# A fused four-layer graph kernel: the set-up before the first tile in another order

## The chip, the cores and the metric

The kernel runs on one NeuronCore of one Trainium2 chip. The metric is the device time of one execution in microseconds, as a median of several runs. The core has a tensor engine (PE; its weight loads are listed apart, as PEld), a vector engine (DVE), a scalar engine (ACT), GpSimd (POOL) and a sync engine (SP) that does nothing but start transfers. Each engine takes its instructions strictly in the order in which they were written for it, and waits where an operand or a buffer isn't ready. ACT can start transfers too; while it does, it computes nothing.

## The reference

For 64 graphs with N = 256 nodes and 128 features, x has the shape 64 x 256 x 128, and all graphs share one 256 x 256 matrix `adj`. Four layers follow one another, each of the form x = x + layer(relu(layernorm(x))). The start of the kernel concerns the first alone:

```python
W1, W2 = (W[:, :F], W[:, F:])          # W is adj, F = 128
s1 = jnp.einsum('bkf,ef->bke', x, W1)
s2 = jnp.einsum('bkf,ef->bke', x, W2)
pre = s1[:, :, None, :] + s2[:, None, :, :] + b_lin
h = jnp.where(pre >= 0, pre, ALPHA * pre)
e = jnp.einsum('bije,e->bij', h, a) + bias   # bias is adj too
attn = jax.nn.softmax(e, axis=2)
out = jax.nn.sigmoid(jnp.einsum('bij,bjf->bif', attn, x))
```

For each graph, e needs 256 x 256 x 256 leaky-relu values, and these pairwise values are most of the kernel's work. The other three layers are a gated graph layer, an attention with tanh and exp, and five steps of a recurrent gate; their weights are the many small inputs (bi, bn, bm, be, We, Wi, Wn, Wm, q, k, v, w3 to u5).

## The kernel before

**Tiling.** The graphs go in groups of one or two. For a graph, h is layer-normed x (`ln_relu`: bn_stats and bn_aggr on DVE, four small operations on POOL for rstd and shift, the relu on ACT), then it is transposed on PE (`transpose_blocks`), and two products with W give s1 (receivers, with the bias b_lin) and s2 (senders). A negative copy of s1, s1n, serves the engines that write the relu as a maximum. `Pairs` then goes through 32 rows of eight receivers each. A batch is eight tiles of 128 x 256; three engines make batches in different forms: ACT by a relu with s1 as bias (L620), POOL by min and max with s1n (L625), DVE by a maximum over a half batch at once (L608). PE multiplies each batch by the window `a_win`, which holds signs, and adds it to `e_ps` (L673). ACT and DVE keep their own copies of s2 in PSUM (`s2_act`, `s2_dve`). The batches lie in ten buffers (`r`); a buffer is free again once PE has read it. Where PE has five batches waiting, a row's second half is merged into the first by DVE (L642), which saves PE a batch.

**Set-up.** The order of W's rows is chosen by the sign of `a`. `constants0` computes it: sgn, then five small matmuls that count signs (`before_ps`), then eight tiny DVE operations that give each row its place, then a scaled permutation matrix `perm` (four DVE operations, L264). Four matmuls apply it to adj (`w_p_ps`), and the result is copied to `w_p`, whose half 0 makes s1 and whose half 1 makes s2. Aside from that way, `a_rep` and `v2_ps` give `v2_rep`, with which each e_ps is opened; `odd_ps` holds the permuted bias and a count, and feeds `blin_p` and `blin_n`; `left_ps` and `bounds` give a correction that the softmax of each graph needs (`adj_l`). `constants1` prepares the later layers' weights.

**Transfers.** Before any of this, the program starts its loads. SP takes x of the first group, x of the second, thirteen weights and x of the third. ACT takes twelve: adj, a, b_lin, bi, bn, the broadcasts of bm and be, and five biases.

**Order.** `tc.manual_schedule()` leaves the order to the code. A planner (the loop at the end) keeps one clock for each engine in nanoseconds, `model.t`, which the priced calls `dve(n)`, `act(n)`, `pool(ns)` and `mm` advance. The work apart from the tiles is in five chains of Python generators: `ahead` (heads and senders of coming graphs), `behind` (softmax), `chain3`, `chain12` and `chain4` (set-up and later layers). Each `yield` names the engine of the next piece, and may name a condition and an earliest time. The loop takes whatever can start earliest by the clocks: a piece of a chain, a half batch of tiles, a merge, or a product of PE. A piece can start when the piece before it in its chain is done, plus a lag (300 ns after PE, 150 DVE, 170 ACT, 200 POOL); if `paced` is set, it also waits for a due time, which grows by the chain's pace (1500 for `ahead`, 2400 for `chain3`) with each piece, from 300 on. Tiles are dealt once `s2` of a graph is in `sent`: from then on, any of ACT, DVE and POOL whose clock is lowest takes the next half batch. So the planner decides on paper; the chip only carries out the order.

All clocks begin at 0, and no clock knows of the time that transfers take to land. Before the change `paced` holds from the first moment (until the last two graphs). The price of a 128 x 256 tile is 357 on ACT and 453 on POOL, a DVE half batch 1131, a batch on PE 858.

Of the kernel before, what the change touches and what calls it, by code (L numbers as in the profile page):

```python
# [8 lines left out]
F32 = mybir.dt.float32  # L9
# [3 lines left out]
P = 128  # L13
# [6 lines left out]
BUFS = 10  # L20
SPARE = 5
MARGIN = {"pe": 300}
MEMORY = 7000
LAG = {"pe": 300, "dve": 150, "act": 170, "pool": 200}

# [5 lines left out]
def sizes(xt):  # L31

    blocks = xt.shape[1]
    return blocks, blocks // 2, blocks * P
# [19 lines left out]
def kernel(ctx: ExitStack, tc: tile.TileContext, ins: dict, out: bass.AP):  # L54
# [18 lines left out]
    def psum(shape, name):  # L73
        return ps_b.tile(shape, F32, tag="ps_b", name=name)
# [4 lines left out]
    def psum_h(shape, name):  # L79
        return ps_h.tile(shape, F32, tag="ps_h", name=name)  # L80
# [17 lines left out]
    def mm(out, lhsT, rhs, **flags):  # L98


        n = 1
        for d in rhs.shape[1:]:
            n *= d
        model.op("pe", max(n, 64) * 1.676)
        for c in range(4):
            nc.tensor.matmul(  # L106
                out[bass.ts(c, 32), :], lhsT=lhsT[:, bass.ts(c, 32)], rhs=rhs, **flags
            )
# [22 lines left out]
    def fetch(shape, name, source, queue=nc.sync, t=None):  # L131
        t = t or constant(shape, name)
        queue.dma_start(out=t, in_=source)
        return t

    def column(name):

        v = ins[name]
        return fetch(
            [P, v.shape[0] // P], "c_" + name, v.rearrange("(c p) -> p c", p=P), nc.scalar  # L140
        )

    order = ctx.enter_context(tc.manual_schedule())
    xts = [load_x(0)]
    adj_n = fetch([P, 2, N], "adj_n", adj.rearrange("(c p) m -> p c m", p=P), nc.scalar)
    a_col = column("L0_gnn_a")
    blin = column("L0_gnn_b_lin")
    ident = constant([P, P], "ident")
    make_identity(nc, ident)
    neg_half = constant([P, 4], "neg_half")  # L150
# [59 lines left out]
    def constants0():  # L210
# [13 lines left out]
        dve(2).scalar_tensor_tensor(a_abs, a_col, -1.0, a_col, ALU.mult, ALU.max)  # L224
        for c in range(2):
            dve(P).tensor_scalar(
                a_rep[:, c, :], a_rep[:, c, :], a_col[:, c : c + 1], None, ALU.mult
            )
# [9 lines left out]
        v2_ps = psum([P, P], "v2_ps")  # L238
        for c in range(2):
            mm(  # L240
                v2_ps, lhsT=adj_n[:, c, P : 2 * P], rhs=a_rep[:, c, :],
                start=(c == 0), stop=(c == 1),
            )
        yield "dve"
        bef = constant([P, 3], "bef")
        dve(3).tensor_copy(bef, before[:, 0:3])
        n_pos = bef[:, 2:3]
# [14 lines left out]
        for src in range(2):  # L262
            for c, size in ((0, a_abs), (1, a_abs1)):
# [13 lines left out]
        act(2 * N).copy(w_p, p)  # L277
        counts["w_p"] += 1
        yield "dve"
        dve(P).tensor_copy(v2_rep, v2_ps)  # L280

# [9 lines left out]
        p = psum([P, 4], "odd_ps")  # L291
        mm(p[:, 0:1], lhsT=ones, rhs=odd, start=True, stop=True)
        for c in range(2):
            for src in range(2):
                mm(
                    p[:, 1 + c : 2 + c], lhsT=perm[:, src, c, :], rhs=blin[:, src : src + 1],
                    start=(src == 0), stop=(src == 1),
                )
        yield "dve"
        dve(2).tensor_copy(blin_p, p[:, 1:3])  # L300
        dve(2).tensor_scalar(blin_n, p[:, 1:3], -1.0, None, ALU.mult)
        counts["w_p"] += 1
        odd_all = constant([P, 1], "odd_all")
        dve(1).tensor_copy(odd_all, p[:, 0:1])
# [101 lines left out]

    def ln_relu(space, xt, tag, ln, when=None):

        G = xt.shape[1]
        for g in range(G):
            if g % 2 == 0:
                yield "dve", when
# [16 lines left out]
        pool(302).tensor_tensor(shift, minus, rstd, ALU.mult)  # L431
        for g in range(G):
            if g % 2 == 0:
                yield "act"
            if g == 0:
                h = space.tile([P, G, P], F32, tag=ln, name=tag, bufs=3 if space is ap else 1)
            act(P, 2, 1).activation(  # L437
                h[:, g, :], xt[:, g, :], AF.Relu, bias=shift[:, g : g + 1],
                scale=rstd[:, g : g + 1],
            )  # L440
        return h

    def transpose_blocks(space, src, tag, banks):
# [8 lines left out]
        act(W).copy(t, tp)  # L452
        return t


    def head(xt, to):
        G, _, W = sizes(xt)
# [47 lines left out]
    def senders(b, of, to):  # L505

        h_t = flat(of["h_t"][:, 2 * b : 2 * b + 2, :])
        yield "pe"
        p = psum_h([P, 2, N], "s2_ps")
        for ec in range(2):  # L510
            mm(p[:, ec, :], lhsT=w_p[:, 1, bass.ts(ec, P)], rhs=h_t, start=True, stop=True)
        yield "act"
        s2 = ap.tile([P, 2, N], F32, tag="s2", name="s2")
        act(2 * N).copy(s2, p)
        to["s2"] = s2
# [13 lines left out]
        to["adj_l"] = adj_l  # L529
# [536 lines left out]
            ahead.add(senders(graphs[n + 1][1], made[graphs[n + 1][0]], sent[n + 1]))  # L1066

    chain3.add(constants0())
    ahead.add(head(xts[0], made[0]))
    ahead.add(senders(0, made[0], sent[0]))  # L1070
    ahead.add(head(xts[1], made[1]))
    n = 0
    while True:
        paced = n < len(graphs) - 2
        if not making and n < len(graphs) and "s2" in sent[n]:
            g, b = graphs[n]
            making.append(Pairs(g, b, made[g], sent[n]))
            multiplying.append(making[0])
            begin(n)
            n += 1  # L1080
# [92 lines left out]
```

## Time and profile before

| What | us |
| --- | --- |
| median of three runs | 5151.03 (5151.01 to 5160.24) |
| the profiled execution, its own time | 5146.78 |
| span of the profiled execution | 5144.3 |
| first product of PE on set-up data (`before_ps`) | 4.89 |
| table load of ACT | 10.18 to 11.46 |
| first tile of ACT, POOL, DVE | 23.59, 23.66, 24.51 |
| last pairwise work, about | 5050 |

The page is read as follows: times are in us from the start of the span; "busy" leaves out time spent in issuing transfers and in waiting. Matmul ends are modelled, so a busy PE is not a PE at its peak. In a line of the order of time, the number in brackets is the time for which the engine stood idle before, and after the arrow stands what ended it. Instructions of one kind that follow one another are one line with a count. PE splits each f32 product in four column groups and two instructions each, so that one `mm` shows as eight.

### The profile page before, as it was taken

How to read it: one execution, taken by the hardware profiler on the slowest of the kernel's cores; microseconds unless marked ns; L12 is line 12 of the kernel's file. 1: busy time of each engine (PE TensorE's matmuls, PEld its weight loads, DVE VectorE, ACT ScalarE, POOL GpSimd, SP SyncE). 2: the span in 40 equal slices, each digit the busy share in tenths (PEclk: the TensorE clock that was granted, in tenths of full speed). 3: DMA queues.
4: the chain of work that ended last, by engine and by line, in shares of the span. 5: the costliest groups of instructions: out<-in, count | busy, mean ns of one | idle time of the engine just before them, and what ended most of it. 6: DMA issues, size and time to landing. Idle time of an engine off the chain costs nothing. (4 is left out here: it accounts for less than half of the span.)

```text
span 5144.3 us, 172484 instructions
## 1 busy us (share of the span) xinstructions
PE 5063.0 (98%) x66800; PEld 2358.0 (46%) x66800; DVE 4983.5 (97%) x9900; ACT 5032.0 (98%) x13224; POOL 4895.6 (95%) x10829
## 2 busy tenths in 40 slices
PE   8999999999999999999999999999999999999997
PEld 4545444436444444544444544544444444444443
DVE  7999999999999999999999999999999999999994
ACT  7999999999999999999999999999999999999994
POOL 8999999999999999999999999999999999999992
PEclk9999999999999999999999999999999999999999
DMA  0000000000000000000000000000000000000000
GB/s 21 6 2 5 5 6 6 6 2 6 6 6 6 2 6 6 6 6 2 6 6 6 6 6 2 6 6 6 6 2 6 6 6 5 2 5 4 4 6 6
DMA packets 56104, 29.32 MB, mean 6 GB/s; under 512 B 20337, under 2 KB 55281, under 8 KB 55281
## 3 DMA queue, kind: packets, MB, share of 16 engines
q1 hardware_dynamic: 53168, 17.97, 1.4%
q8 instruction: 522, 8.55, 0.7%
q14 instruction: 302, 2.47, 0.2%
q10 hardware_dynamic: 2112, 0.33, 0.0%
HBM read 9.84 MB, written 8.45 MB: 4 GB/s over the span
## 5 line engine op out<-in xcount | busy, mean ns | idle before, releaser
L625 POOL TENSOR_SCALAR r<-s,s1n 128x256 f32<-128x256 f32 x10204 | 4646.4, 478 | 102.0 <-PE e_ps L673 33.5
L620 ACT ACTIVATE r<-s_act,s 128x256 f32<-128x256 f32 x9976 | 4593.6, 1478 | 10.5 <-PE e_ps L673 10.4
L673 PE MATMUL e_ps<-r,a_win 128*32 128x512 f32 x27632 | 3379.5, 593 | 9.8 <-POOL r L625 3.4
L642 DVE SCALAR_TENSOR_TENSOR r<-s_dve,s1n,r 128x256 f32<-128x256 f32 x5136 | 2093.8, 471 | 2.0 <-ACT r L620 1.0
L608 DVE TENSOR_TENSOR r<-s_dve,s1n 128x1024 f32<-128x1024 f32 x1735 | 2017.3, 1210 | 7.3 <-PE e_ps L673 1.4
L673 PEld LDWEIGHTS e_ps<-r,a_win 128*32 128x32 f32 x27632 | 1095.3, 110 | 1593.2 <-issue 1124.2
L620 ACT ACTIVATE r<-s,s 128x256 f32<-128x256 f32 x512 | 381.1, 1666 | 0.0
L437 ACT ACTIVATE h<-x,bsh,brs 128x128 f32<-128x128 f32 x384 | 329.8, 1386 | 3.6 <-POOL bsh L431 2.3
L946 ACT ACTIVATE gate_ps<-gate_ps,bz 128x512 f32<-128x512 f32 (+1 forms) x170 | 269.7, 1586 | 5.9 <-PE gate_ps L106 5.9
L948 ACT ACTIVATE hv_ps<-hv_ps,bh 128x512 f32<-128x512 f32 (+1 forms) x170 | 266.4, 1567 | 5.4 <-PE hv_ps L106 5.4
L106 PE MATMUL m_ps<-adj_t,hn 128*32 128x256 f32 x4096 | 268.1, 380 | 2.8 <-ACT hn L968 2.7
L927 ACT COPY m_t<-m_ps 128x512 f32<-128x512 f32 (+1 forms) x170 | 260.9, 1535 | 8.5 <-PE m_ps L106 8.5
L933 ACT ACTIVATE m_ps<-gate_ps,br 128x512 f32<-128x512 f32 (+1 forms) x170 | 256.9, 1511 | 9.2 <-PE gate_ps L106 8.8
L968 ACT COPY hn<-hn_ps 128x512 f32<-128x512 f32 (+1 forms) x136 | 208.1, 1530 | 20.6 <-PE hn_ps L106 20.5
L106 PEld LDWEIGHTS m_ps<-adj_t,hn 128*32 128x32 f32 x4096 | 157.5, 110 | 112.3 <-issue 31.9
L697 ACT ACTIVATE pm<-e_ps,nmax 128x256 f32<-128x256 f32 x128 | 195.0, 1531 | 2.2 <-DVE nmax L688 2.2
L106 PE MATMUL gate_ps<-m_t,t_w_w 128*32 128x512 f32 (+1 forms) x1360 | 187.3, 572 | 8.6 <-ACT m_t L927 7.8
L106 PE MATMUL gate_ps<-m_t,w_t 128*32 128x512 f32 (+1 forms) x1360 | 185.2, 568 | 3.1 <-ACT m_ps L933 3.1
L106 PE MATMUL hv_ps<-m_t,t_w_w 128*32 128x512 f32 (+1 forms) x1360 | 185.0, 567 | 0.0
L106 PE MATMUL hv_ps<-rh,u_th 128*32 128x512 f32 (+1 forms) x1360 | 184.9, 567 | 0.0
L106 PE MATMUL hn_ps<-ident,hf 128*32 128x128 f32 x4096 | 162.9, 274 | 12.5 <-DVE hf L958 12.5
L106 PEld LDWEIGHTS hn_ps<-ident,hf 128*32 128x32 f32 x4096 | 136.4, 110 | 77.0 <-issue 51.3
(206 smaller groups left out, 5951.7 us busy)
## 6 DMA issues: line engine op xcount, KB each, us to landing
xt<-in_x_dram SPq DMA_DIRECT2D x30, 256.0 KB
out_dram<-y SPq DMA_DIRECT2D x30, 256.0 KB
row<-rows SPq DMA_DIRECT2D x128, 0.5 KB
xt<-in_x_dram SPq DMA_DIRECT2D x4, 128.0 KB
out_dram<-y SPq DMA_DIRECT2D x4, 128.0 KB
bound<-row SPq DMA_DIRECT2D x30, 2.0 KB
raw_L_gnn_w_w<-in_L_gnn_w_w_dram SPq DMA_DIRECT2D x3, 128.0 KB
adj_n<-in_adj_dram ACTq DMA_DIRECT2D x1, 256.0 KB
```

The lines of the kernel that those rows point to most:

```text
L106: nc.tensor.matmul(out[bass.ts(c, 32), :], lhsT=lhsT[:, bass.ts(c, 32)], rhs=rhs, **flags)
L437: act(P, 2, 1).activation(h[:, g, :], xt[:, g, :], AF.Relu, bias=shift[:, g : g + 1], scale=rstd[:, g : g + 1],)
L608: nc.vector.tensor_tensor(r[:, 2 * g2 : 2 * g2 + 2, :, :], s2[:, ec : ec + 1, :].unsqueeze(1).to_broadcast([P, 2, 2, N]), self.s1n_v[:, ec ...
L620: nc.scalar.activation(r[:, g, ic, :], s2[:, ec, :], AF.Relu, bias=s1[:, ec, i : i + 1])
L625: nc.gpsimd.tensor_scalar(r[:, g, ic, :], s2[:, ec, :], FLT_MAX, s1n[:, ec, i : i + 1], ALU.min, ALU.max,)
L642: nc.vector.scalar_tensor_tensor(r[:, g, ic, :], self.own("dve")[:, 1, :], self.of["s1n"][:, 1, i : i + 1], r[:, g, ic, :], ALU.max, ALU.add,)
L673: nc.tensor.matmul(self.e_ps[bass.ts(g, 32), :, :].rearrange("p a b -> p (a b)"), lhsT=a_win[:, batch["ec"], 31 - t : 63 - t], rhs=flat(r[ ...
L927: act(W).copy(m_t, m_ps)
L933: act(W, 1).activation(t_r, g_ps, AF.Tanh, bias=br, scale=0.5)
L946: act(W, 1).activation(t_z, g_ps, AF.Tanh, bias=bz, scale=0.5)
L948: act(W, 1).activation(cand, hv_ps, AF.Tanh, bias=bh)
L968: act(W).copy(hn, tp)
```

## The change

Four things are moved, and the planner's start is set in another way.

- **Transfers.** `column` and the two broadcasts go to SP's queue. ACT keeps two: a, which is now first, and adj. b_lin is second on SP, after x of the first group; the other nine stay at their places in the program, behind most of the weights.
- **Table.** A one-column tanh on ACT, on a constant set by DVE, stands right after ACT's two transfers.
- **W.** In `constants0` the a_rep products and `v2_ps` move behind W; the permuted bias gets its own bank and its matmuls stand ahead of W's; W's matmuls run half 1 first; its copy is split in two, one for each half.
- **First group.** `first_head` takes the place of `head` and of the first part of `senders` for the first group: it makes s2 and s1 by four matmuls into two banks, with one wait for the whole of W; s1n is made by DVE, s2 and s1 by ACT.
- **Planner.** x of the first group is taken to land at 3400 ns and a at 3900. Nothing is paced before the first graph's tiles begin. At that moment the clocks of all engines are raised to ACT's.

```diff
-    def column(name):
+    def column(name, queue=nc.sync):
...
     xts = [load_x(0)]
+    a_col = column("L0_gnn_a", nc.scalar)
     adj_n = fetch([P, 2, N], "adj_n", adj.rearrange("(c p) m -> p c m", p=P), nc.scalar)
-    a_col = column("L0_gnn_a")
     blin = column("L0_gnn_b_lin")
+    table = constant([P, 1], "table")
+    nc.vector.memset(table, 0.0)
+    nc.scalar.activation(table, table, AF.Tanh)
...
-    bm_bc = fetch([P, P], "bm_bc", ins["L1_gnn_bm"].partition_broadcast(P), nc.scalar)
-    be_bc = fetch([P, 1], "be_bc", ins["L1_gnn_be"].partition_broadcast(P), nc.scalar)
+    bm_bc = fetch([P, P], "bm_bc", ins["L1_gnn_bm"].partition_broadcast(P))
+    be_bc = fetch([P, 1], "be_bc", ins["L1_gnn_be"].partition_broadcast(P))
...
-        yield "dve"
+        yield "dve", None, LANDS + 500
...
         yield "pe"
+        b_ps = psum([P, 2], "blin_ps")
+        for c in range(2):
+            for src in range(2):
+                mm(
+                    b_ps[:, c : c + 1], lhsT=perm[:, src, c, :], rhs=blin[:, src : src + 1],
+                    start=(src == 0), stop=(src == 1),
+                )
         p = psum([P, 2, N], "w_p_ps")
-        for half in range(2):
+        for half in (1, 0):
...
-        yield "act"
-        act(2 * N).copy(w_p, p)
-        counts["w_p"] += 1
+        yield "dve"
+        dve(2).tensor_copy(blin_p, b_ps)
+        dve(2).tensor_scalar(blin_n, b_ps, -1.0, None, ALU.mult)
+        for half in (1, 0):
+            yield "act"
+            act(N).copy(w_p[:, half, :], p[:, half, :])
+        counts["w_p"] += 2
+        yield "dve"
+        for c in range(2):
+            dve(P).tensor_scalar(
+                a_rep[:, c, :], a_rep[:, c, :], a_col[:, c : c + 1], None, ALU.mult
+            )
+        yield "pe"
...
+    def first_head(xt, to, snd):
+
+        G, _, W = sizes(xt)
+        h = yield from ln_relu(ap, xt, "h0", "h0", at=LANDS)
+        h_t = yield from transpose_blocks(ap, h, "h0t", psum_h)
+        to.update(h=h, h_t=h_t)
+        yield "pe", lambda: counts["w_p"] > 1
+        s2_ps, s1_ps = psum_h([P, 2, N], "s2_ps"), psum_a([P, 2, W], "s1_ps")
+        for half, p in ((1, s2_ps), (0, s1_ps)):
+            for ec in range(2):
+                mm(
+                    p[:, ec, :], lhsT=w_p[:, half, bass.ts(ec, P)], rhs=flat(h_t),
+                    start=True, stop=True,
+                )
+        yield "dve"
+        s1n = ap.tile([P, 2, W], F32, tag="s1n", name="s1n")
+        for ec in range(2):
+            dve(W, 1).tensor_scalar(
+                s1n[:, ec, :], s1_ps[:, ec, :], -1.0, blin_n[:, ec : ec + 1], ALU.mult, ALU.add
+            )
+        yield "act"
+        s2 = ap.tile([P, 2, N], F32, tag="s2", name="s2")
+        act(2 * N).copy(s2, s2_ps)
+        s1 = ap.tile([P, 2, W], F32, tag="s1", name="s1")
+        for ec in range(2):
+            act(W, 1).activation(
+                s1[:, ec, :], s1_ps[:, ec, :], AF.Identity, bias=blin_p[:, ec : ec + 1]
+            )
+        to.update(s1=s1, s1n=s1n)
+        snd["s2"] = s2
...
-    ahead.add(head(xts[0], made[0]))
+    ahead.add(first_head(xts[0], made[0], sent[0]))
...
-        paced = n < len(graphs) - 2
+        paced = 0 < n < len(graphs) - 2
...
             making.append(Pairs(g, b, made[g], sent[n]))
+            if n == 0:
+                model.t = {e: max(t, model.t["act"]) for e, t in model.t.items()}
```

More of the change, by code (lines that the diff above doesn't have):

```diff
@@ L22 @@
 MARGIN = {"pe": 300}
+LANDS = 3400
 MEMORY = 7000
@@ L134, in fetch @@
         return t
-    def column(name):
+    def column(name, queue=nc.sync):
         v = ins[name]
-        return fetch(
-            [P, v.shape[0] // P], "c_" + name, v.rearrange("(c p) -> p c", p=P), nc.scalar
-        )
+        return fetch([P, v.shape[0] // P], "c_" + name, v.rearrange("(c p) -> p c", p=P), queue)
     order = ctx.enter_context(tc.manual_schedule())
     xts = [load_x(0)]
+    a_col = column("L0_gnn_a", nc.scalar)
     adj_n = fetch([P, 2, N], "adj_n", adj.rearrange("(c p) m -> p c m", p=P), nc.scalar)
-    a_col = column("L0_gnn_a")
     blin = column("L0_gnn_b_lin")
+    table = constant([P, 1], "table")
+    nc.vector.memset(table, 0.0)
+    nc.scalar.activation(table, table, AF.Tanh)
     ident = constant([P, P], "ident")
@@ L219, in col @@
             return constant([P, 2], name)
-        yield "dve"
+        yield "dve", None, LANDS + 500
         sgn, a_abs = col("sgn"), col("a_abs")
         dve(2).tensor_scalar(sgn, a_col, 0.0, None, ALU.is_ge)
[L224 to L228, printed above, removed]
         yield "pe"
@@ L235, in constants0 @@
         mm(before[:, 2:3], lhsT=ones, rhs=sgn[:, 1:2], start=False, stop=True)
[L238 to L243, printed above, removed]
         yield "dve"
+        dve(2).scalar_tensor_tensor(a_abs, a_col, -1.0, a_col, ALU.mult, ALU.max)
         bef = constant([P, 3], "bef")
@@ L275, in constants0 @@
                 )
-        yield "act"
-        act(2 * N).copy(w_p, p)
-        counts["w_p"] += 1
+        yield "dve"
[11 more added lines that the diff above has]
+        yield "pe"
+        v2_ps = psum([P, P], "v2_ps")
+        for c in range(2):
+            mm(
+                v2_ps, lhsT=adj_n[:, c, P : 2 * P], rhs=a_rep[:, c, :],
+                start=(c == 0), stop=(c == 1),
+            )
         yield "dve"
@@ L290, in constants0 @@
         yield "pe"
[L291 to L298, printed above, removed]
+        p = psum([P, 1], "odd_ps")
+        mm(p, lhsT=ones, rhs=odd, start=True, stop=True)
         yield "dve"
-        dve(2).tensor_copy(blin_p, p[:, 1:3])
-        dve(2).tensor_scalar(blin_n, p[:, 1:3], -1.0, None, ALU.mult)
-        counts["w_p"] += 1
         odd_all = constant([P, 1], "odd_all")
-        dve(1).tensor_copy(odd_all, p[:, 0:1])
+        dve(1).tensor_copy(odd_all, p)
         left, left_n, left_nb = col("left"), col("left_n"), col("left_nb")
@@ L405, in constants1, with ln_relu @@
                 dve(1).tensor_scalar(t, t, scale, None, ALU.mult)
-    def ln_relu(space, xt, tag, ln, when=None):
+    def ln_relu(space, xt, tag, ln, when=None, at=None):
         G = xt.shape[1]
@@ L413, in ln_relu @@
             if g % 2 == 0:
-                yield "dve", when
+                yield "dve", when, at
             if g == 0:
@@ L453, in transpose_blocks @@
         return t
+    def first_head(xt, to, snd):
[7 more added lines that the diff above has]
+            for ec in range(2):
+                mm(
+                    p[:, ec, :], lhsT=w_p[:, half, bass.ts(ec, P)], rhs=flat(h_t),
[14 more added lines that the diff above has]
+                s1[:, ec, :], s1_ps[:, ec, :], AF.Identity, bias=blin_p[:, ec : ec + 1]
+            )
+        to.update(s1=s1, s1n=s1n)
+        snd["s2"] = s2
     def head(xt, to):
@@ L507, in senders @@
         h_t = flat(of["h_t"][:, 2 * b : 2 * b + 2, :])
[L508 to L515, printed above, removed]
+        if "s2" not in to:
+            yield "pe"
+            p = psum_h([P, 2, N], "s2_ps")
+            for ec in range(2):
+                mm(p[:, ec, :], lhsT=w_p[:, 1, bass.ts(ec, P)], rhs=h_t, start=True, stop=True)
+            yield "act"
+            s2 = ap.tile([P, 2, N], F32, tag="s2", name="s2")
+            act(2 * N).copy(s2, p)
+            to["s2"] = s2
         if "bound" not in of:
```

## The prediction, made before the change was run

> **What bounds the kernel now.** I read the page first, then the first 60 us in order of time, engine by engine, then busy time by stretch and the waits of the first 60 us. The page says that the long middle is full:
>
> ```profile
> PE 5063.0 (98%) x66800; PEld 2358.0 (46%) x66800; DVE 4983.5 (97%) x9900; ACT 5032.0 (98%) x13224; POOL 4895.6 (95%) x10829
> ```
>
> Four engines share one job, so a change can gain only where they are not full: at the two ends. The diff touches only the start. The order of time gives the way to the first tile on ACT, DVE and POOL (columns: start us, us, engine, line, operation, count, idle before and its releaser):
>
> ```profile
> 9.81 0.33 ACTq L133 DMA_DIRECT2D c_L_gnn_u_b<-in_L_gnn_u_b_dram  x1
> 10.18 1.28 ACT L437 ACT_TABLE_LOAD   x1 [10.18 <-DMA c_L_gnn_w_b<-in_L_gnn_w_b_dram]
> 11.47 0.88 ACT L437 ACTIVATE h<-xt,bsh,brs 128x128 f32<-128x128 f32 x2
> 16.58 0.58 ACT L277 COPY w_p<-w_p_ps 128x512 f32<-128x512 f32 x1 [3.04 <-PE w_p_ps L106]
> 22.97 0.59 ACT L514 COPY s<-s_ps 128x512 f32<-128x512 f32 x1 [2.05 <-PE s_ps L106]
> 23.66 29.06 POOL L625 TENSOR_SCALAR r<-s,s1n 128x256 f32<-128x256 f32 x63 [16.82 <-ACT s L514]
> 24.51 3.48 DVE L608 TENSOR_TENSOR r<-s_dve,s1n 128x1024 f32<-128x1024 f32 x3
> ```
>
> ACT issues transfers until 10.14, loads its table, and only then makes h, whose shift POOL had ready at 6.84. PE sits behind h (transposes at 12.02), although the permutation was ready at 8.43. Production starts at 23.6.
>
> The second loss comes after that. Busy time by stretch (sum, instructions in brackets), and the waits of 23.6 to 60:
>
> ```profile
> 23.60:60.00 36.40, 32.95 (x288) 11.73 (x284) 26.19 (x50) 22.24 (x60) 35.99 (x80) 0.95 0.01 2
> 140.00:5050.00 4910.00, 4874.89 (x64286) 2260.15 (x64282) 4840.43 (x9636) 4890.03 (x12858) 4773.89 (x10545) 1.00 0.02 5
> ```
>
> ```profile
> PEld e_ps L673 <- POOL r L625: 16.6, 19, 3.1
> ACT h L437 <- POOL bsh L431: 8.0, 1, 8.0
> DVE adj_t L342 <- PE adj_t_ps L106: 7.3, 1, 7.3
> ```
>
> The columns are PE, PEld, DVE, ACT, POOL. In 36.4 us ACT was idle 14.2 us, DVE 10.2, POOL 0.4; everybody waits for POOL. The planner's clocks explain it. In them nothing before the first tile costs POOL more than the layer norm: due at 3.3 us, 1.8 long, so POOL is free at 5.1, while the same plan has ACT at 20.3 (s2 copy due at 300 + 13 x 1500 ns = 19.8 us) and DVE at 18.0 (due at 300 + 7 x 2400 ns = 17.1, and 0.9 of work). It therefore deals POOL some 15 us of tiles before s2 exists. In truth all three begin at 23.6: POOL is 18.6 us behind its plan, DVE 5.6, ACT 3.3, and PE's fixed order makes the others wait for the difference, 13 and 15 us, which is about the 10.2 and 14.2 idle.
>
> **What the skill says.** "ScalarE: Activation LUTs", What ACT_TABLE_LOAD costs: about 1283 ns a load, plus a drain on a switch. The trace has 1.28 us, once. "DMA: Bandwidth & Descriptors", Issuing engines are not separate DMA queues: a second issuing engine saves only sequencer time. The trace agrees: ACT's loss is issue time. "TensorE: Matmul & The Clock Gate", Part 1: half clock until about 3.4 us of sustained work. Here PE worked from 12.02, its weight loads still came 0.43 us apart per four at 15.44 (the half-rate pace of 256 columns), by 17.22 they were faster, and the granted clock was 0.50 again at 21 to 26. So "about 4 to 5 us" in this trace.
>
> **The change, part by part, up to the first tile.** Order on each engine follows from the planner's own prices, now without due times before the first graph.
>
> 1. ACT's queue: ten of twelve transfers go to SP; ACT keeps the a vector (now first) and adj. That frees ACT from about 1.7 instead of 10.14; table and dummy tanh end by about 3.3, hidden under the wait for x (first bn_stats at 3.49). Cost nothing; uncovered it would be 1.3 + 0.2. On SP the ten add between 10 x 0.33 = 3.3 us and the 8.4 they took on ACT (1.76 to 10.14): the last load goes out at 15.8 to 20.9 instead of 12.5. Queued behind: x(1), first read at 46.9 before; bm's broadcast, read by DVE at 46.2; the row transfer of the bounds at 29.2. All have over 8 us of cover; if it were gone, DVE would stall in order at bm's addition. b_lin, second on SP, is wanted at 8.1.
> 2. sgn waits for x's statistics (3.98) and for a, issued 0.71 instead of 1.24 (landing took 3.3 us): 4.05 instead of 4.57. sgn to bef took 1.09, bef to the end of perm 2.77: perm is done at 7.91. Moving the two a_rep products and V2's matmuls (0.47, 1.09) behind changes little here, they lay beside the wait.
> 3. Layer norm in parallel: aggregates at about 4.3, POOL 1.4, h at about 6.3 to 7.2. By the plan W's matmuls (6.5) now stand ahead of h's transposes (7.2), so h waits on PE.
> 4. PE from 8.1: b_lin's 0.45, W's four at 0.91 (3.64/4, half clock): 12.2. Halving W buys nothing here, since h comes last anyway. Transposes 0.85 (0.43 if warm), hop 0.25, copy 0.37, second half of W 0.30: 13.9 (13.5).
> 5. s2 and s1 on two banks: four matmuls without ACT between, 0.86 each at half clock or 0.43 warm, plus 0.25: done at 17.6 or 15.5. In the old kernel the same took from 17.16 to 22.9. The new wait (both halves copied) has V2 and then odd behind it on PE; V2 is wanted only by the first batch.
> 6. DVE's s1n, 0.47 for the last: POOL starts at 16.2 to 18.1, I take 17.2; ACT, with s2's copy under the s1 matmuls, 17.3; DVE has v2, a_win and odd first (1.02) and its own copy of s2 (0.89): 19.1.
>
> First loss: POOL 6.5 us earlier, ACT 6.3, DVE 5.4. A batch takes POOL 8 x 0.461 = 3.69 us, ACT 8 x 0.372 = 2.98, DVE 2 x 1.16 = 2.32, so 0.271 + 0.336 + 0.431 = 1.04 batches per us. Gain (6.5 x 0.271 + 6.3 x 0.336 + 5.4 x 0.431)/1.04 = **6.0 us**; ends 4.8 (cold) and 7.0 (warm).
>
> Second loss: all planner clocks are set to ACT's at the first graph, so POOL gets no head start. What was lost, (14.2 x 0.336 + 10.2 x 0.431 + 0.4 x 0.271)/1.04 = **8.9 us**, comes back, but for two things. PE is cold as the first batches come at about 20.8: 1.71 instead of 0.86 us a batch for 4 to 5 us leaves it some two batches behind, of ten buffers; I charge 0.6. The odd/left work (DVE 0.7, PE about 2.5) is now done during production: 0.3. Ends: nothing recovered, or all.
>
> That chain is next at 300 + 2400 x 10 = 24.3 in plan time, left done at 31.5, adj_l from 40.3, about 44.5 on the chip; it was 45.0. The first softmax wants it after the whole first graph, so nothing is late there.
>
> Sum: 6.0 + 8.9 - 0.6 - 0.3 = **14.0**. The profiled execution took 5146.8 (5144.3 of span, 2.5 around it): 5132.8. The median of the runs is 4.2 higher: 5151.0 - 14.0 = **5137.0**. As a check by the plan: at the planner's prices ACT's clock stands at 14.05 at the first graph (s1n ends at 12.73, lag 0.15, then 1.18 for s2 and s1), and so do all. DVE's first tile is planned at 14.7 and comes at 19.1, so the largest lag falls from 18.6 to about 4.4, and the plan, whose mean start moves from 15.3 to 14.05, ends about 1 us sooner: 15.2 before the cold PE.
>
> **Rivals.**
> A. Only the first tile moves, and the idle after it stays or turns into waits on a cold PE: 6 us, 5145. For: PE's half clock at 20 to 26 will come again, with three producers at once. Against: the clocks' skew fits the idle of ACT and DVE to within 3 us.
> B. The list of all 64 graphs is dealt anew, as the planner is greedy and starts from other clocks. Place: 140 to 5050, where ACT was idle 4910 - 4890.0 = 20 us (0.41%), DVE 70, POOL 136. If ACT's idle rose to 34 the gain is gone, from 44 (0.9%) on the kernel is over 0.2% slower; I put it at 5163. For: single waits of POOL there reach 6.0 us, so local misfits exist. Against: the old deal kept ACT at 99.6% over some 60 graphs, with the same prices and the same tiles.
> C. PE warm at s1, or a better deal: 5128. For: PE will have worked from 8.1 without a gap. Against: its window was slow to open before.
> D. The change doesn't do what it says: were a's transfer or PE's order no better, production would start at 22 or later. The landing times speak against; it is in A's chance.
>
> **How the numbers follow.** The likeliest (5137, own range 5131 to 5144) has 0.62, four fifths of it beyond 0.2% (10.3 us, about what the measurement can tell from no change); C 0.13, all beyond; A 0.14, within; B 0.11, of it 0.09 slower. Faster 0.50 + 0.13 = 0.63, same 0.12 + 0.14 + 0.02 = 0.28, slower 0.09. The range 5125 to 5153 leaves out the worse part of B and the far end of C, under 2 in 10.
>
> **What would show it.** Table load at about 1.8; sgn at 4.0; W's matmuls ahead of h's transposes, from 8.1; POOL's first tile at 16 to 18, DVE's at 18 to 20; ACT's and DVE's idle from the first tile to 60 down to 3 us or less; ACT's idle in 140 to 5050 still 15 to 30 us. Wrong if the transposes stand first, if SP's row transfer is held by loads, if a second table load appears, or if the steady stretch loses what the start gains.

## The result, and the profile after

The changed kernel takes 5145.08 us (median of ten runs, 5139.71 to 5149.44), the kernel before 5158.78 (ten runs, 5151.01 to 5163.77). The ratio is 0.9975, with a 95% interval of 0.9966 to 0.9983: 13 us, or a quarter of a per cent, faster. The forecast was 14.0 us, so the size and the sign came true; the time forecast, 5137.0, is 8 us low because the median of three runs that it started from lies 8 us under that of ten.

The profiled executions don't show this gain at their ends: the changed kernel's took 5148.91, the one of before 5146.78. Why that is so comes out of the first experiment. What they do show is the start. The changed kernel's page, line of the engines:

```profile
PE 5044.3 (98%) x66664; PEld 2367.0 (46%) x66664; DVE 5023.1 (98%) x9997; ACT 5043.4 (98%) x13248; POOL 4922.5 (96%) x10837
```

The shares hardly moved: DVE from 97% to 98%, POOL from 95% to 96%, ACT stayed at 98%. Lines from the first 17 us of the changed kernel in order of time (start us, us, engine, line, operation, count, idle before and its releaser):

```profile
1.77 1.28 ACT L149 ACT_TABLE_LOAD   x1 [1.77 <-issue]
3.61 0.15 DVE L225 TENSOR_SCALAR sgn<-c_L_gnn_a 128x2 f32<-128x2 f32 x1
5.44 0.88 ACT L443 ACTIVATE h<-xt,bsh,brs 128x128 f32<-128x128 f32 x2 [2.17 <-POOL bsh L437]
7.67 3.55 PE L107 MATMUL w_p_ps<-perm,adj_n 128*32 128x256 f32 x32
11.04 0.62 PE L107 MATMUL h0t_ps<-ident,h 128*32 128x128 f32 x16
12.15 1.93 PE L107 MATMUL s_ps<-h0t,w_p 128*32 128x256 f32 x32 [0.49 <-ACT h0t L458]
15.22 25.02 POOL L663 TENSOR_SCALAR r<-s,s1n 128x256 f32<-128x256 f32 x55 [9.81 <-DVE v_rep L295]
16.80 12.53 DVE L646 TENSOR_TENSOR r<-s_dve,s1n 128x1024 f32<-128x1024 f32 x11
```

W's matmuls start at 7.67 instead of 12.87, ahead of h's transposes and not behind them. The four products for s2 and s1 follow one another in 1.93 us. POOL's first tile comes at 15.22 instead of 23.66, DVE's at 16.80 instead of 24.51, ACT's at 15.85 instead of 23.59.

Busy time of the same two stretches as before (PE, PEld, DVE, ACT, POOL, instructions in brackets), and all that ACT waited for between its first tile and 60 us:

```profile
23.60:60.00 36.40, 36.06 (x430) 17.31 (x426) 36.26 (x54) 35.90 (x101) 35.20 (x78) 1.00 0.03 5
140.00:5050.00 4910.00, 4847.35 (x63973) 2268.20 (x63970) 4860.98 (x9714) 4880.72 (x12823) 4794.47 (x10540) 1.00 0.02 5
```

```profile
ACT rows L531 <- PE bound_ps L526: 0.5, 1, 0.5
```

ACT's idle in the first stretch fell from 14.2 us to 0.5, DVE's from 10.2 to 0.1. In the long stretch ACT was idle 29 us where it had been 20 (21 and 13 in the second profiles of the two kernels).

To follow the lead between the start and the end I use the loads of x. SP starts one as a group begins, and the loads stand in the same sequence in every version. Below, "the third" and "the last" are the 3rd and the 30th of the loads after 40 us.

### The profile page after: what moved, and what is told of

The parts are those of the page before. It is cut to its first block, busy times and chain, and to the rows that moved or that the text cites. A ratio compares the mean times of both kernels' runs of the same rounds, so it can differ in the third digit from the quotient of the medians.

```text
span 5146.6 us, 172388 instructions
## 1 busy us (share of the span) xinstructions
PE 5044.3 (98%) x66664; PEld 2367.0 (46%) x66664; DVE 5023.1 (98%) x9997; ACT 5043.4 (98%) x13248; POOL 4922.5 (96%) x10837
## 5 line engine op out<-in xcount | busy, mean ns | idle before, releaser
L658 ACT ACTIVATE r<-s_act,s 128x256 f32<-128x256 f32 x10000 | 4513.4, 1300 | 6.1 <-PE e_ps L711 5.7
L680 DVE SCALAR_TENSOR_TENSOR r<-s_dve,s1n,r 128x256 f32<-128x256 f32 x5272 | 2152.1, 471 | 4.0 <-ACT r L658 3.6
L646 DVE TENSOR_TENSOR r<-s_dve,s1n 128x1024 f32<-128x1024 f32 x1693 | 1965.1, 1211 | 6.8 <-PE e_ps L711 0.5
L443 ACT ACTIVATE h<-x,bsh,brs 128x128 f32<-128x128 f32 x384 | 301.9, 1202 | 5.2 <-POOL bsh L437 5.2
L965 ACT COPY m_t<-m_ps 128x512 f32<-128x512 f32 (+1 forms) x170 | 233.2, 1372 | 17.2 <-PE m_ps L107 17.2
L984 ACT ACTIVATE gate_ps<-gate_ps,bz 128x512 f32<-128x512 f32 (+1 forms) x170 | 241.3, 1420 | 4.9 <-PE gate_ps L107 4.7
L986 ACT ACTIVATE hv_ps<-hv_ps,bh 128x512 f32<-128x512 f32 (+1 forms) x170 | 239.8, 1411 | 4.5 <-PE hv_ps L107 4.5
L971 ACT ACTIVATE m_ps<-gate_ps,br 128x512 f32<-128x512 f32 (+1 forms) x170 | 232.6, 1368 | 11.8 <-PE gate_ps L107 8.2
L735 ACT ACTIVATE pm<-e_ps,nmax 128x256 f32<-128x256 f32 x128 | 162.2, 1267 | 4.8 <-DVE nmax L726 4.8
```

Source lines behind the costliest of these rows:

```text
L443: act(P, 2, 1).activation(h[:, g, :], xt[:, g, :], AF.Relu, bias=shift[:, g : g + 1], scale=rstd[:, g : g + 1],)
L646: nc.vector.tensor_tensor(r[:, 2 * g2 : 2 * g2 + 2, :, :], s2[:, ec : ec + 1, :].unsqueeze(1).to_broadcast([P, 2, 2, N]), self.s1n_v[:, ec ...
L658: nc.scalar.activation(r[:, g, ic, :], s2[:, ec, :], AF.Relu, bias=s1[:, ec, i : i + 1])
L680: nc.vector.scalar_tensor_tensor(r[:, g, ic, :], self.own("dve")[:, 1, :], self.of["s1n"][:, 1, i : i + 1], r[:, g, ic, :], ALU.max, ALU.add,)
L965: act(W).copy(m_t, m_ps)
L971: act(W, 1).activation(t_r, g_ps, AF.Tanh, bias=br, scale=0.5)
```

## The experiments

**The kernel before once more, and the changed kernel once more.** Both are unchanged.

> The kernel before, unchanged, profiled once more. Marks: first POOL tile (23.66 in the first profile), the load of x at 197.59, the last load of x at 4501.89. In the two profiles at hand the changed kernel leads by 15 us at the second mark and by only 5 at the third. Theory 1: the lead is lost because the first profile of before was of a quick execution (5146.8, below all the later runs); then the first two marks come again within 1 us, and the last load comes at 4508 to 4514. Theory 2 (rival B of the prediction: the new deal of tiles loses in the long stretch): all three marks come again within 2 us.

> The changed kernel, unchanged. First POOL tile at 15.2, the load of x at 182.1, the last load of x near 4497 by both theories (4494 to 4500 if executions differ by a rate); a time of 13 us under before.

Measured: ratios 0.9999 (0.9990 to 1.0007) and 0.9970 (0.9958 to 0.9981), medians 5159.53 and 5144.29 us. The gain came again. All ratios here and below are to the kernel before, run beside the version in question. The third and the last load of x, in the kernel before (first profile), the kernel before (second profile) and the changed kernel (second profile), one fence each:

```profile
197.59 0.39 SPq L121 DMA_DIRECT2D xt<-in_x_dram  x1
4501.89 0.51 SPq L121 DMA_DIRECT2D xt<-in_x_dram  x1
```

```profile
197.79 0.40 SPq L121 DMA_DIRECT2D xt<-in_x_dram  x1
4510.14 0.51 SPq L121 DMA_DIRECT2D xt<-in_x_dram  x1
```

```profile
183.44 0.40 SPq L122 DMA_DIRECT2D xt<-in_x_dram  x1
4499.55 0.50 SPq L122 DMA_DIRECT2D xt<-in_x_dram  x1
```

One program, two executions: 0.2 us apart at the third load, 8.3 us at the last, 13.9 us at the end (spans 5144.3 and 5158.2). So the first profile of before caught a quicker execution, as theory 1 had it, and the changed kernel did not lose its lead. Against the second profile the lead is 14.4 us at the third load, 10.6 at the last and 15.5 at the end. The groups of instructions show one rate that differs clearly, POOL's tiles. The two executions of before:

```profile
L625 POOL TENSOR_SCALAR r<-s,s1n 128x256 f32<-128x256 f32 x10204 | 4646.4, 478 | 102.0 <-PE e_ps L673 33.5
```

```profile
L625 POOL TENSOR_SCALAR r<-s,s1n 128x256 f32<-128x256 f32 x10204 | 4671.0, 505 | 91.1 <-PE e_ps L673 29.1
```

Busy time over count is 455.3 ns a tile in the quick one and 457.8 in the other. That is half a per cent; whether it causes the 13.9 us or goes with them is not shown. The profiles of all versions fall into these two paces. Seven have 457.1 to 457.8 ns: the second of before, both of the changed kernel, and those with the clocks alone, without the clocks' line, with 4000 ns and with four extra products. The other seven have 455.3 or 455.4. In what follows the third load, which came only 0.2 us apart in these two executions, is compared between all versions; the end of a profile is compared only with that of another of the same pace, and times otherwise by ratios.

The changed kernel's own first tile and third load moved as well: 16.05 and 183.44 where 15.2 and 182.1 were expected. The order is the same, but in the second profile PE made the transposes and the products for s2 and s1 more slowly (0.62 and 1.93 us in the first):

```profile
11.08 1.09 PE L107 MATMUL h0t_ps<-ident,h 128*32 128x128 f32 x16
12.65 2.25 PE L107 MATMUL s_ps<-h0t,w_p 128*32 128x256 f32 x32 [0.48 <-ACT h0t L458]
```

**The planner's clocks alone**, in the kernel before:

```diff
             multiplying.append(making[0])
+            if n == 0:
+                model.t = {e: max(t, model.t["act"]) for e, t in model.t.items()}
```

> The kernel before, with only the planner's clocks raised to ACT's when the first graph begins. Theory (the idle of ACT and DVE until 60 us comes from POOL's head start on paper): first tiles still at 23.6 to 24.5; idle of ACT from the first tile to 60 falls from 14.2 to under 4, of DVE from 10.2 to under 4; the load of x at 197.6 comes 7 to 10 us sooner (188 to 190); the time falls by 6 to 10 us. Rival (the idle is that of a half-clock PE and of full buffers): idle stays over 10 and 8, the load at 195 to 198, time within 3 us of before.

Measured: ratio 1.0003 (0.9995 to 1.0011), no gain where 6 to 10 us were expected. Busy time from 23.6 to 60 us, columns as above, and the two loads:

```profile
23.60:60.00 36.40, 34.27 (x429) 22.70 (x425) 34.82 (x50) 35.63 (x98) 35.09 (x77) 0.92 0.04 10
```

```profile
188.54 0.39 SPq L121 DMA_DIRECT2D xt<-in_x_dram  x1
4509.15 0.51 SPq L121 DMA_DIRECT2D xt<-in_x_dram  x1
```

The idle is gone (ACT 0.8 us, DVE 1.6), and the third load comes 9.3 us sooner than in the second profile of before: up to there the theory holds. At the last load 1.0 us of it is left, and in the time nothing. POOL's tiles took 457.7 ns here and 457.8 there, so the pace isn't the reason; the 9 us were given back bit by bit in the long stretch (5.7 us of lead at the tenth load, 4.2 at the twentieth), with another deal of tiles.

**The clocks' line taken out** of the changed kernel:

```diff
-            if n == 0:
-                model.t = {e: max(t, model.t["act"]) for e, t in model.t.items()}
```

> The changed kernel without the line that raises the planner's clocks. On paper POOL is then free at 6.1 and ACT at 14.05, on the chip both begin at 15.2 to 15.9, so POOL is 7 to 8 us further behind its plan than ACT, not 15. Theory: first tiles as in the changed kernel (15.2 to 16.8), idle of ACT until 60 about 7 and of DVE about 6, the load of x at 182 comes some 5 us later (186 to 188), time 3 to 6 us above the changed kernel. Rival: the clocks' line is worth nothing once the start is quick: idle under 3, the load at 182 to 183.

Measured: ratio 0.9977 (0.9968 to 0.9986), median 5147.16 us. From 23.6 to 60 ACT was idle 6.0 us, about as expected, and DVE 2.9, half of it, but the third load came at 183.28, no later than with the line: the expected 5 us fell. The median is 2.9 us above that of the changed kernel beside it (5144.29), and the intervals of the two ratios overlap, so its worth in the time isn't clear of nothing.

**POOL's head start put back**, in the changed kernel, in two sizes (4000 and 15000 ns):

```diff
                 model.t = {e: max(t, model.t["act"]) for e, t in model.t.items()}
+                model.t["pool"] -= 15000
```

> The changed kernel with POOL's clock on paper set 4000 ns behind the other three as the first graph begins, so that POOL is dealt about one batch more and ACT and DVE less. It tests whether a new deal of the tiles by itself moves the time (rival B). Theory: first tiles and their times as in the changed kernel; ACT idle until 60 grows by 1 to 4 us, ACT gets some 10 fewer tiles (3.7 us), the time within 3 us. Rival B: the time moves by 5 us or more either way, with the change of ACT's idle and of its tiles adding up to it.

> The changed kernel with POOL's clock on paper set 15000 ns behind as the first graph begins: the head start that the kernel before gave POOL, with the quick start of the changed one. It measures the price of the head start by itself. Theory (the prediction's second loss): ACT idle until 60 is 11 to 14 us, DVE idle 7 to 10, the load of x at 183 comes 4 to 9 us later, the time rises by 4 to 9 us against the changed kernel (ratio to before 0.9980 to 0.9990). Rival (POOL waits 100 us later anyway, so tiles dealt to it early cost nothing in the end, as the run with 4000 ns and the run without the clocks' line suggest): idle appears and the load is late, but the ratio stays within 0.996 to 0.9977.

Measured: with 4000 ns a ratio of 0.9960 (0.9948 to 0.9972), ACT idle 2.4 us from 24 to 60, 28 fewer tiles for it, the third load at 186.51, 3 us late; with 15000 ns 0.9969 (0.9957 to 0.9981). The latter's busy time from 23.6 to 60, two of its waits between 15.2 and 60, its third load, and that of the run without the dummy tanh (below), which ran beside it with the changed kernel's deal:

```profile
23.60:60.00 36.40, 36.40 (x343) 14.95 (x346) 28.01 (x44) 26.41 (x72) 36.40 (x80) 1.00 0.01 2
```

```profile
PEld e_ps L711 <- POOL r L663: 18.8, 27, 0.8
ACT r L658 <- PE e_ps L711: 6.1, 5, 2.0
```

```profile
190.58 0.40 SPq L122 DMA_DIRECT2D xt<-in_x_dram  x1
```

```profile
182.81 0.40 SPq L122 DMA_DIRECT2D xt<-in_x_dram  x1
```

This is the picture of the kernel before, made on purpose: PE waits for POOL's tiles, ACT waits for PE, ACT is idle 10.0 us and DVE 8.4, and the third load comes 7.1 us later than in the second profile of the changed kernel, 7.8 later than in the run beside it. And yet the ratio is that of the changed kernel, and the two profiles side by side, both at the pace of 455 ns, end 0.3 us apart (spans 5139.1 and 5138.8). The theory holds for the start, the rival for the time.

The ratio with 4000 ns is the lowest of all. Its interval overlaps those of the changed kernel (0.9970 and 0.9975). But two versions with the changed kernel's deal ran beside it on the same chip, the one with the transfers back and the one with four extra products (both below); their ratios are 0.9984 and 0.9982, with intervals that begin (0.9977 and 0.9974) above the end of its own (0.9972). At the same pace its span is 8.0 us shorter than that of the version with four extra products (5139.7 against 5147.7), though its third load came 3.2 us later; that version's later first tile, 0.9 us, is too little for that. So there rival B came true: a deal changed at the start moved the end by some 7 us, this time for the better.

**A late start with the same deal.** Twelve memsets that the planner doesn't price, on DVE's way to the permutation:

```diff
         dve(2).tensor_scalar(sgn, a_col, 0.0, None, ALU.is_ge)
...
         yield "dve"
+        for _ in range(12):
+            nc.vector.memset(idle, 0.0)
```

> The changed kernel with twelve memsets of a spare tile on DVE behind sgn, which the planner doesn't price: the order on every engine stays as it was, but the permutation, W and the first tile come about 6 us later (first tile of POOL at 21 to 22). It measures the price of the first tile's moment by itself, with the same deal of tiles. Theory: one for one; all loads of x come 5.5 to 6.5 us later (the load at 183 at 189), the time rises by 6 us against the changed kernel (ratio to before 0.9982 to 0.9987). Rival: slack further on takes up a late start; the loads of x close up to within 2 us by the end and the ratio stays at 0.9970 to 0.9975.

Measured: first tile of POOL at 22.64, the third load at 189.47, 6.0 us behind the second profile of the changed kernel and 6.7 behind the run without the dummy tanh, which ran beside it with the same deal. That much is one for one. The ratio is 0.9984 (0.9976 to 0.9992), 5 to 7 us above that of the changed kernel, as expected. But the intervals overlap, and the run below with the transfers back on ACT has the same ratio without the delay. In the two profiles side by side, both at the pace of 455.3 ns, the delay closed to nothing at the last load (4495.35 against 4496.13) and was 1.4 us at the end. So how much of a late start reaches the end stays open. One thing is shown: with the first tile only about 1 us sooner than in the second profile of before, this version leads by 8.3 us at the third load and by 8 us in the time. With this deal a gain that is hardly that of the first tile does last.

**The old head** for the first group, one half of s1 after the other through one bank, and s2 last:

```diff
-    ahead.add(first_head(xts[0], made[0], sent[0]))
+    ahead.add(head(xts[0], made[0], LANDS))
```

> The changed kernel with the first group made by the old head and senders (one s1 half after the other through one bank, s1n by ACT, s2 last), all else as changed. Theory: from the copy of W to the first tile it takes again about 6.4 us as in the kernel before (17.2 to 23.6) instead of 3.0 to 3.6, so POOL's first tile comes at 18 to 19.5, and the load of x at 182 to 183 comes 2 to 4 us later. Rival: the old order overlaps with the copies and costs under 1 us.

Measured: the transposes behind W's products begin at 11.09, as in the changed kernel, but s2 is copied only at 20.89 and POOL starts at 21.58, worse than expected. Part of its order of time:

```profile
17.62 1.08 PE L107 MATMUL left_ps<-left_rep,adj_n 128*32 128x128 f32 x16 [1.30 <-DVE left_rep L317]
18.89 1.94 PE L107 MATMUL s_ps<-h0t,w_p 128*32 128x256 f32 x16
20.89 0.58 ACT L552 COPY s<-s_ps 128x512 f32<-128x512 f32 x1 [3.91 <-PE s_ps L107]
```

With nothing paced before the first tile, the side chain for `left` gets in front of s2. The third load comes at 184.09, only 0.7 us after the changed kernel's second profile, where 2 to 4 were expected, though the first tile is 5.5 us later. That the work of `left` is then already done may be part of the reason; the deal of tiles is another one too (5176 merges where the changed kernel has 5272), and which of the two it is isn't shown. Ratio 0.9986 (0.9979 to 0.9992).

**The transfers back on ACT's queue**, behind the table load; the order of all else is the same:

```diff
-    def column(name, queue=nc.sync):
+    def column(name, queue=nc.scalar):
...
-    be_bc = fetch([P, 1], "be_bc", ins["L1_gnn_be"].partition_broadcast(P))
+    be_bc = fetch([P, 1], "be_bc", ins["L1_gnn_be"].partition_broadcast(P), nc.scalar)
```

> The changed kernel with the ten small loads (columns and the two broadcasts) back on ACT's queue, behind the table load; the planner's order is the same. Theory (the prediction's step 1: ACT's issue time was on the way): ACT is free only at about 10.2 to 10.5, h comes then instead of at 5.4; but in the new order W's matmuls run on PE until 11.2, so h's transposes start at about 11.4 instead of 11.0 and POOL's first tile comes 0 to 1 us later (15.2 to 17), the time within 3 us of the changed kernel. Rival (ACT's transfers were what the first tile waited for): first tile 4 us later or more, at 19 to 20, time 4 us up or more.

Measured, in order of time:

```profile
7.66 3.37 PE L107 MATMUL w_p_ps<-perm,adj_n 128*32 128x256 f32 x32
11.37 0.88 ACT L443 ACTIVATE h<-xt,bsh,brs 128x128 f32<-128x128 f32 x2 [7.58 <-DMA c_L_gnn_u_b<-in_L_gnn_u_b_dram]
11.91 0.81 PE L107 MATMUL h0t_ps<-ident,h 128*32 128x128 f32 x16 [0.89 <-ACT h L443]
```

ACT makes h 5.9 us later, and it costs POOL's first tile 0.2 to 1.1 us (16.28 against 16.05 and 15.22), the third load nothing (183.10). W's products on PE cover ACT's transfers now. Ratio 0.9984 (0.9977 to 0.9992), against 0.9970 and 0.9975 for the same order of tiles. The intervals overlap, and the profile can't settle it: it is of an execution at the pace of 455.3 ns, 20 us below this version's median. The run was also on another chip than the changed kernel's second one, and the version with four extra products, which ran beside it with the same deal, has about the same ratio (0.9982). Whether the chip makes the difference isn't shown. I take some 5 us as the size below which two versions that didn't run beside each other can't be told apart here.

**No dummy tanh.**

```diff
-    nc.scalar.activation(table, table, AF.Tanh)
```

> The changed kernel without the dummy tanh. Theory: the table load waits only for ACT's queue and still runs at about 1.8, in the wait for h, so h comes at 5.4 and the first tile where it was (15.2 to 16.1). Rival: the load stands directly before h's relu, in its wait for POOL; h comes 1.3 us later, at 6.7, still ahead of its transposes at 11.0, and the first tile doesn't move either. Only the place of the load tells them apart.

Measured: the load stands at 3.27, behind the landing of x, and ends long before h's relu can run. The first tile comes at 15.98, between those of the changed kernel's two profiles. The time of the one run, at the pace of 455.3 ns, is 5141.5 us. The load didn't go to 1.8, as the theory had it, nor into the wait for POOL just before the relu, as the rival had it; either way the dummy buys nothing at the first tile.

```profile
3.27 1.28 ACT L442 ACT_TABLE_LOAD   x1 [3.27 <-DMA xt<-in_x_dram]
```

**More work for PE before W**, to raise its clock: products of constants into a spare bank, which nobody reads (`warm` is one product of 256 columns in its four column groups), two and two, then three and three.

```diff
+    warm()
+    warm()
...
         mm(before[:, 2:3], lhsT=ones, rhs=sgn[:, 1:2], start=False, stop=True)
+        warm()
+        warm()
```

> The changed kernel with four extra products of constants on PE (two before the counts, two between the counts and the permutation), read by nobody, so that PE works from 1.6 us on. Theory (the prediction's term of 0.91 us for each of W's four products is the half clock): W's four take 1.8 to 2.2 us in place of 3.55, POOL's first tile comes 1.3 to 1.8 us sooner, at 13.5 to 14.7. Rival: gaps between the small products keep the clock at half; nothing moves, or the first tile comes up to 0.8 us later.

> As the run with four extra products on PE, but six, three and three, so that PE works on wide products from 1.6 to 4.2 and from about 4.9 to 7.4, with only the narrow counting products between. In the run with four the clock stayed at half until 12 or later. Theory (narrow products and gaps don't count as work for the clock; two wide stretches of 2.6 us may be too short as well): W's four still take 3.4 us or more, and the first tile comes 0.3 to 1 us later than in the changed kernel. Rival (it is the sum of the work): W's four take 1.8 to 2.3 us, the first tile at 14.3 to 15.

Measured, lines of PE in order of time, with four and with six:

```profile
4.50 1.95 PE L216 MATMUL warm_ps<-left_rep 128*32 128x256 f32 x16
6.84 0.29 PE L107 MATMUL blin_ps<-c_L_gnn_b_lin,perm 128*32 128x1 f32 x8 [0.40 <-DVE perm L268]
7.74 3.64 PE L107 MATMUL w_p_ps<-perm,adj_n 128*32 128x256 f32 x32
```

```profile
1.61 2.79 PE L216 MATMUL warm_ps<-left_rep 128*32 128x256 f32 x24 [1.61 <-DVE left_w L163]
4.72 1.99 PE L216 MATMUL warm_ps<-left_rep 128*32 128x256 f32 x24
7.91 1.93 PE L107 MATMUL w_p_ps<-perm,adj_n 128*32 128x256 f32 x32
```

Both theories missed, in opposite ways, and the rivals held in the main. With four, W stayed at half clock (3.64 us) and the first tile at 16.18; ratio 0.9982 (0.9974 to 0.9990). With six, the second three already took 1.99 us where the first took 2.79, W took 1.93, and POOL's first tile came at 13.83, 1.4 to 2.2 us sooner than in the changed kernel. So the 0.91 us for each of W's products, 0.48 here, was the half clock, as the prediction said. The third load came at 181.11, 1.7 us before that of the run without the dummy tanh beside it; the spans, at the same pace, are 5138.2 and 5138.8, which shows no gain at the end.

## Why the prediction was right, and where it wasn't

**Right: the order.** W's matmuls stand ahead of h's transposes, from 7.67 (forecast 8.1 for the bias, which began at 6.77). Table load at 1.77 (1.8), DVE's own copy behind v2, a_win and odd, the row transfer of the bounds not held up (36.94). The forecast that halving W buys nothing is in line with the trace: the first half's copy ended at 11.66, and PE waited for h's copy until 12.15. The 0.30 us that the prediction added for the second half were not on the way: that copy ran from 11.99 to 12.37, beside the first products of s2. The ten transfers delayed SP less than it reckoned: the last load was out at 14.96, not at 15.8 to 20.9.

**First loss: right in kind, 6.0 us forecast, 7.1 to 7.9 measured.** By the same sum, with first tiles at 15.22, 15.85 and 16.80, it is (8.4 x 0.271 + 7.7 x 0.336 + 7.7 x 0.431)/1.04 = 7.9, and 7.1 with those of the second profile (16.05, 16.68, 17.63). Two terms were too long. sgn was put at 4.05 by the old landing time of a, 3.3 us from issue; a had landed by 3.61, at most 2.9 us. And s2 and s1 ran at the full clock in the first profile, 1.93 us in all, and for the most part in the second, 2.25, where I took the middle of the warm and the cold case (1.7 and 3.4). The late-start run shows the price at the third load, one for one.

**Second loss: right until the third load, wrong as a term of the sum.** The lead there is 14.4 to 15.5 us; less the first loss, 7.3 to 7.6 remain for POOL's head start, where 8.9 - 0.6 - 0.3 = 8.0 was forecast. The clocks alone gave 9.3 at that place, the head start put back cost 7.1 to 7.8. But the prediction let this gain stand until the end, and as a part it doesn't do so reliably: the late start kept some 8 us with hardly a sooner first tile, but the clocks alone leave the time where it was (1.0003, 0.9995 to 1.0011), and putting the head start back costs nothing (0.9969). The step that failed is "comes back, but for two things". It left out the long stretch, which is dealt anew whenever the clocks differ at the start. Nor are the two terms separate: without the clocks' line the changed kernel keeps 12 us of its gain and the whole lead at the third load. The quick start, which also halves POOL's head start, is then worth about twice the 6.0 us that the prediction gave the first tile, and the clocks' line some 3 us by the medians instead of 8.

**Rival B was put too low.** It named the place, the long stretch, and the size, a loss of all the gain or more, and the parts showed such sizes: 9 us lost for the clocks alone, and 7 us won for the head start of 15000 ns, between the third load and the end. Its mark didn't show it: ACT's idle in the long stretch grew by 8 us with the clocks alone (13 to 21), but by as much in the changed kernel, which lost nothing. What in a deal makes it good or bad isn't settled. One price can be read: a tile that DVE merges takes it 0.41 us, one of a half batch 0.29. By the prediction's sum, and as an estimate that leaves out what PE saves, the 176 further merges with the clocks alone cost 176 x 0.12 x 0.431/1.04 = 8.7 us, about what was lost. But the same estimate gives the changed kernel a loss of 6.8 that it doesn't show, and the count of merges doesn't sort the versions (5312 with the clocks alone, 5272 in the changed kernel, 5136 before, 5096 with 4000 ns of head start, 4936 with 15000). The changed kernel's deal neither gained nor lost much, so the sum came out. That it did is partly luck: for a part of this change alone the same working would have been off by 9 us.

**Parts that carried little.** With W first on PE, the ten transfers moved to SP are worth 0.2 to 1.1 us of the first tile, and the dummy tanh nothing. The prediction had both on its list of hidden or freed costs but didn't say that step 3 covers step 1. ACT's issue time was what the old order waited for; the new order of PE hides it.

**Rival A** (the idle stays, with a cold PE) fell: the clock was granted at 0.80 from 15.2 to 23.6 in the first profile and at 1.00 in the second, full afterwards in both, and ACT's idle went to 0.5 us. **Rival C**'s mechanism, PE warm at s1, happened; with the earlier `sgn` it is the difference in the first loss.

What stays open: how much of the first tile's moment reaches the end, and with it how the 13 us split. The quick start without the clocks' line has nearly the whole gain (0.9977), the clocks alone none, and the late start took 5 to 7 us back by the ratios, but 1.4 us between two profiles. Two parts of the change were not run alone: W ahead of the transposes, and the start without due times.

## What to carry to other kernels

Where a planner deals out a long list from clocks that it keeps itself, look at how far each engine is from its own plan at the moment the list begins; the idle that follows was about the difference of these lags here, and the first tiles in the order of time give it. But a gain at the start of such a list is a gain only if the list stays the same: measure it by a mark soon after the start and by the time at the end, and expect that a new deal can move the end by as much as the gain. And before a cost is taken off the critical path, ask which other part of the change would have covered it.

## What the runs showed of the hardware that was not expected

The same order of instructions ran at two paces: 5144.3 and 5158.2 us of span for the kernel before, with POOL's tiles at 455.3 and 457.8 ns. The profiles with the transfers back and with the old head, at 455.3 ns too, were of executions 20 us below the median of their own version; that with the head start of 15000 ns, at 455.4, was not below it (5140.97 and 5140.99). So two single profiles a quarter of a per cent apart say little about two kernels where the pace of POOL's tiles isn't the same.

In the run with four extra products PE's clock did not open, that is, go from half to full, for two stretches of 1.9 us of wide products with gaps of 0.4 us around narrow ones; in that with six it opened about 4 us after the start of a stretch without gaps (2.79 us at half clock, 0.5 us of one-column products, then 1.99 us for the same three products, which would take 1.45 at the full clock, by W's 1.93 for four). But the moment isn't fixed by the order of the work: in the changed kernel's two profiles PE began the stretch that holds W's products at 7.29 and 7.30, and the transposes at 11.04 took 0.62 us in one, those at 11.08 took 1.09 in the other. This agrees with the Trainium skill, "TensorE: Matmul & The Clock Gate", Part 1, which speaks of about 3.4 us of sustained work in a window that runs freely, so that the moment varies. Here that was worth 0.8 us of the first tile (15.22 and 16.05).

The table load waited for less than the activation it served: without the dummy it ran at 3.27, when x had landed, 2.2 us before h, which needed POOL's shift and scale as well, could start at 5.45. With the dummy, the tanh followed the load at once (1.77 + 1.28, then 3.07).
